# Gram stages of a two-block ResNet bottleneck: transposes moved from TensorE to a way through DRAM and VectorE

## The chip, the cores and the metric

The kernel runs on one core of one Trainium2 chip. The metric is the device time of one execution in microseconds (us), the median of several runs. The engines are TensorE (PE, matrix products and transposes into PSUM), VectorE (DVE), ScalarE (ACT), GpSimd (POOL) and SyncE (SP, which only issues DMA transfers). They run independently and wait for each other through semaphores.

## The reference

Two bottleneck blocks follow each other on x of shape (64, 1024, 14, 14), float32. Each block is

```python
out = relu(bn(conv(x, w1, b1, 1, 0), g1, be1))      # 1x1, 1024 -> 256
out = relu(bn(conv(out, w2, b2, 1, 1), g2, be2))    # 3x3, 256 -> 256
out = bn(conv(out, w3, b3, 1, 0), g3, be3)          # 1x1, 256 -> 1024
out = softplus(residual_scale)[0] * out
return relu(x + out)
```

`bn` takes mean and variance over all 64 x 196 = 12544 pixels of each channel in this very batch. So no normalisation can start before its convolution has ended for the whole batch, and the third convolution would have to be computed twice, or its output kept, unless its statistics are known ahead.

## The kernel before

All data are float32. 256 middle channels are two halves of 128 partitions (MS = 2), 1024 outer channels are eight (CS = 8). The batch is cut into T = 32 tiles of two images, PX = 392 pixels each. The output of the first convolution, and in its place that of the second, stays on the chip for the whole batch in `y_all`, 128 partitions x 2 x 12544.

The stages in order, with the times of the profile: the first convolution of block 0 (0 to 313 us); for each block the second convolution `conv2` (a Winograd form, 313 to 597 and 1340 to 1615), the Gram stage `gram` with `conv3_stats` behind it, and then the third convolution with the residual. For block 0 the latter is `fused` with the first convolution of block 1 (to 1340), for block 1 it is `final` (to the end).

The **Gram stage** finds the mean and variance of the third convolution without computing it. With z the normalised output of the second convolution (256 values per pixel), the variance of w3.z follows from the 256 x 256 matrix of the sums of z.z^T over pixels and the sums of z. `gram` (L855 on) goes through NT = 49 pairs of pixel tiles (2 x 128 pixels). For each it transposes four 128x128 blocks of `y_all` on TensorE into one PSUM bank (L885), VectorE copies the bank to an SBUF tile `zt` and takes off a row `crow` on the way (L887; this keeps the numbers small, c being relu of the norm's shift be2), and TensorE adds the products of the pair to two PSUM banks `g0` and `g1` (L867 and L868; a column of ones gives the sums). The products of a pair stand behind the transposes of the next. ScalarE normalises `y_all` in place ahead of it, group by group of GPX = 1568 pixels (`norm`, L487).

`conv3_stats` (L899 to L938) turns `g0`, `g1` and w3 into mean and variance of all 1024 channels; `affine` makes scale and shift of them; `residual` does tile 0.

Beside the Gram stage of block 0, GpSimd prepares the Winograd **filters** of block 1: four pieces (`filters`, L160 on; `piece` in the main loop), one per pair of channel halves, each with a load of w2, some 35 small operations (L171 to L206) and six stores to DRAM `us`. The filters of block 0 are prepared by VectorE in the first stage, half a piece per step of the first convolution (L1115 to L1124). Near the end of each Gram stage VectorE also makes sums and differences of w1 and w3 (`combine`, L135 to L142).

What sets the order: the program's order is a priority only. A planner with a model of the instructions' durations orders each engine's queue when the program is built; only where the code asks for it (`keep_in_program_order`: the convolutions' matmuls at L158, the activations at L278) is the order fixed. On the chip each engine works through its queue in that order and stops at an instruction whose data are not there. Tiles of a pool with the same tag share a number of buffers; a load into one waits until its last reader is done. SyncE issues most loads, ScalarE and GpSimd some; a transfer counts as landed when all of it is.

Of the kernel before, what the change touches and what calls it, by code (L numbers as in the profile page):

```python
# [33 lines left out]
FP = mybir.dt.float32  # L36
AF = mybir.ActivationFunctionType
ALU = mybir.AluOpType
# [13 lines left out]
CH = 2  # L52
NT = NPX // (CH * P)
NZT = 4

# [25 lines left out]

NROW = M


@with_exitstack
def bottlenecks(ctx: ExitStack, tc: tile.TileContext, x, w1s, w2s, w3s, pars, out):
# [7 lines left out]
    y_grp = y_all.rearrange("p s (g h l) -> p s g h l", g=NG, h=H)  # L94
    mids = [dram.tile([P, CS * PX], FP, tag=f"mid{t}", name=f"mid{t}") for t in range(T)]
    us = [
        [dram.tile([P, MS, MS, NKS[i], P], FP, tag=f"u{b}_{i}", name=f"u{b}_{i}") for i in range(NF)]
# [28 lines left out]

    def load_w1(pool, b):

        w = pool.tile([P, MS, 2, CS // 2, P], FP, tag="w1", name=f"w1_{b}")
        for h in range(2):  # L130
            for o in range(MS):
                nc.scalar.dma_start(out=w[:, o, h], in_=w1s[b][:, o, h])
        return w

    def combine(pool, name, a):  # L135

        s = [pool.tile(a[0][0].shape, FP, tag=f"{name}s{i}", name=f"{name}s{i}") for i in range(4)]
        tc.keep_in_program_order(nc.vector.tensor_add(s[0], a[1][0], a[1][1]))
        nc.vector.tensor_sub(s[1], s[0], a[0][0])
        tc.keep_in_program_order(nc.vector.tensor_sub(s[2], a[0][0], a[1][0]))  # L140
        nc.vector.tensor_sub(s[3], a[0][1], s[1])
        return a, s  # L142
# [13 lines left out]
    def matmul(*args, **kw):  # L156

        tc.keep_in_program_order(nc.tensor.matmul(*args, **kw))  # L158

    def filters(eng, b, s, o, spare):  # L160
# [24 lines left out]
        for i, (row, more, op, by) in parts.items():  # L185
# [23 lines left out]
            nc.gpsimd.dma_start(out=us[b][i][:, s, o], in_=u)  # L209
            if i == 2:  # L210
                yield

# [641 lines left out]

    def gram(psum, pool, aff, crow, beside):  # L855


        g0, g1 = psum.tile(M + 1, "cp"), psum.tile(P + 1, "ap")
        zts = [pool.tile([P, CH, M + 1], FP, tag=f"zt{i}", name=f"zt{i}") for i in range(NZT)]
        for zt in zts:  # L860
            nc.gpsimd.memset(zt[:, :, M:], 1.0)
        normed = 0

        def products(k, zt):
            for c in range(CH):
                first, last = k == 0 and c == 0, k == NT - 1 and c == CH - 1
                nc.tensor.matmul(g0, zt[:, c, 0:P], zt[:, c, :], start=first, stop=last)  # L867
                nc.tensor.matmul(g1, zt[:, c, P:M], zt[:, c, P:], start=first, stop=last)  # L868

        before = None  # L870
        for k in range(NT):
            while normed < NG and normed * GPX < (k + 3) * CH * P:

                px = [normed * GPX, (normed + 1) * GPX]
                if normed == 0:
                    px.insert(1, CH * P)
                for a, b in zip(px, px[1:]):
                    for s in range(MS):
                        norm(s, y_all[:, s, a:b], aff)
                normed += 1  # L880
            tp = psum.tile(CH * M)
            for c in range(CH):
                px = slice((k * CH + c) * P, (k * CH + c + 1) * P)
                for s in range(MS):
                    nc.tensor.transpose(tp[:, (c * MS + s) * P : (c * MS + s + 1) * P], y_all[:, s, px], ident)  # L885
            zt = zts[k % NZT]
            nc.vector.tensor_tensor(  # L887
                zt[:, :, :M], tp.rearrange("p (c m) -> p c m", c=CH),
                crow[:, None, :].to_broadcast([P, CH, M]), ALU.subtract,
            )  # L890
            if before is not None:
                products(*before)
            if k in beside:
                beside[k]()
            before = k, zt
        products(*before)
        return g0, g1

    def conv3_stats(psum, one, grams, w3, ccol, mv):  # L899

# [6 lines left out]
        nc.vector.tensor_scalar(off, g0[:, P:M], 2.0, None, ALU.mult)  # L907

        m = one.tile([P, MS, 2], FP, tag="zmean", name="zmean")
        for s, d in ((0, g0[:, M:]), (1, g1[:, P:])):  # L910
            nc.vector.tensor_copy(m[:, s, 1:2], d)
            nc.vector.tensor_add(m[:, s, 0:1], d, ccol[:, s : s + 1])
        quad = psum.tile(3 * CS, "ax").rearrange("p (o k) -> p o k", k=3)
        ones = one.tile([P, 1], FP, tag="ones", name="ones")
# [13 lines left out]
        for o in range(CS):  # L928
            for s in range(MS):
                matmul(quad[:, o, 0:2], w3[:, s, o, :], m[:, s, :], start=(s == 0), stop=(s == MS - 1))  # L930
        for o in range(CS):
            matmul(quad[:, o, 2:3], q[:, 0, o * P : (o + 1) * P], ones, start=True, stop=True)
        r = small.tile([P, CS, 3], FP, tag="quad", name="quad")
        nc.vector.tensor_copy(r, quad)
        nc.vector.tensor_copy(mv[:, :, 0], r[:, :, 0])
        sq = small.tile([P, CS], FP, tag="sq", name="sq")
        nc.vector.tensor_mul(sq, r[:, :, 1], r[:, :, 1])
        nc.vector.tensor_sub(mv[:, :, 1], r[:, :, 2], sq)  # L938

# [157 lines left out]
    with tc.tile_pool(name="first", bufs=1) as one, tc.tile_pool(  # L1097
        name="first_x", bufs=4
    ) as xpool, ExitStack() as scope:
        psum = Psum(scope, ["ps"], ps=4, ay=2)  # L1100
        w1 = load_w1(one, 0)
        pair = [load_x(xpool, 0, t, 4 if t == 0 else 2) for t in range(2)]
        for b in range(2):
            p = keep.tile([P, NPAR], FP, tag=f"par{b}", name=f"par{b}")
            nc.scalar.dma_start(out=p, in_=pars[b][:, :NPAR])
            par.append(p)
        masks.make_identity(nc, ident)
        w1 = combine_w1(one, w1)

        for t, xt in enumerate(pair):  # L1110
            plain_conv1(psum, t, xt, w1[0], par[0], stats1)


        spare = [y_all[:, i, NPX - CS * PX :] for i in range(MS)]
        quarters = itertools.product(range(MS), range(MS))  # L1115
        work = itertools.chain.from_iterable(
            itertools.chain(filters(nc.vector, 0, s, o, spare), (None,)) for s, o in quarters
        )

        def items():  # L1120
            for t in range(2, T, 2):
                xs = [load_x(xpool, 0, t + i) for i in range(2)]
                yield Conv1(psum, one, xs, (t, t + 1), w1, par[0], stats1)
                next(work, None)  # L1124

        for _ in stream(items()):
            pass

    for b in range(2):
        pb = par[b]  # L1130
        sp = softplus(pb)
        ccol = keep.tile([P, MS], FP, tag="ccol", name="ccol")
        nc.vector.tensor_scalar(ccol, pb[:, BE2 : BE2 + MS], 0.0, None, ALU.max)
        aff = affine(aggregate(stats1, T - 3 + b), MS, pb, G1, BE1)
# [4 lines left out]
        with tc.tile_pool(name=f"last_{b}", bufs=1) as one, tc.tile_pool(  # L1139
# [3 lines left out]
            if b == 0:  # L1143
                w1 = load_w1(one, b + 1)
            aff = affine(aggregate(stats2, 0), MS, pb, G2, BE2)
            with ExitStack() as scope:
# [4 lines left out]
                with tc.tile_pool(name=f"gram_{b}", bufs=1) as pool:  # L1151
                    crow = pool.tile([P, M], FP, tag="crow", name="crow")
                    nc.sync.dma_start(out=crow, in_=pars[b][:, NPAR:])
                    tc.keep_in_program_order(nc.vector.tensor_scalar(crow, crow, 0.0, None, ALU.max))

                    def piece(s, o):
                        spare = [xpool.tile([P, CS * PX], FP, tag="x", name="spare") for i in range(2)]
                        for _ in filters(nc.gpsimd, 1, s, o, spare):
                            pass

                    weights = []

                    def combined():
                        if b == 0:
                            weights.append(combine_w1(one, w1))
                        weights.append(combine_w3(one, w3))

                    beside = {NT - 5: combined}
                    if b == 0:
                        beside.update({1 + 12 * i: partial(piece, i // MS, i % MS) for i in range(MS * MS)})  # L1170
                    grams = gram(psum, pool, aff, crow, beside)
                    made = [conv3(psum, 0, o, w3) for o in range(2)]
                    mv3 = small.tile([P, CS, nc.vector.BN_AGGR_DIM], FP, tag="mv3", name="mv3")
                    conv3_stats(psum, pool, grams, w3, ccol, mv3)
                aff = affine(mv3, CS, pb, G3, BE3, conv_bias=B3)
# [51 lines left out]
```

## Time and profile before

The median is 2053.04 us of 3 runs (2052.73 to 2053.37). The profiled execution has a span of 2048.9 us.

| engine | busy us | share of the span |
|---|---|---|
| TensorE, matmuls | 1988.1 | 97% |
| TensorE, weight loads | 1679.1 | 82% |
| VectorE | 1559.7 | 76% |
| ScalarE | 906.4 | 44% |
| GpSimd | 664.2 | 32% |

| stage | from, to (us) | what is on TensorE |
|---|---|---|
| Gram stage of block 0 | 612 to 708 | transposes and products of 49 pairs |
| statistics, start of `fused` | 708 to 749 | `conv3_stats`, tile 0, first convolutions |
| Gram stage of block 1 | 1630 to 1722 | the same 49 pairs |
| statistics, start of `final` | 1722 to 1747 | as above |

How to read the profile: a group of instructions is given by its line, engine, operation and tile (out<-in), the number, the busy time in us and the mean of one in ns, and the idle time of the engine just before them with what ended it. The times of matmuls overlap, so a sum of them is more than the time they take; the distance from one to the next is the price. "PEclk" is the clock granted to TensorE, 1.00 being full. The chain of waits follows the work that ended last back from the end, at each step to what released it.

### The profile page before, as it was taken

What the parts mean: (1) busy time and instruction counts of PE and PEld (TensorE: products, weight loads), DVE (VectorE), ACT (ScalarE), POOL (GpSimd) and SP (SyncE); (2) the same over time, 40 slices, a digit from 0 to 9 for tenths busy, and PEclk for the clock granted to TensorE, in tenths of its full rate; (3) what the DMA queues carried; (4) which work ended last, traced back from release to release, by engine and by line L of the source; (5) the groups of instructions that cost most, each with busy time, mean ns of one, the idle gap of its engine ahead of it and who ended that gap; (6) DMA issues with size and microseconds to landing.
All of it is one profiled execution on the core that took longest, in us unless ns stands there. A gap on an engine that the chain in (4) does not pass through costs nothing.

```text
span 2048.9 us, 27957 instructions
## 1 busy us (share of the span) xinstructions
PE 1988.1 (97%) x9896; PEld 1679.1 (82%) x9896; DVE 1559.7 (76%) x2892; ACT 906.4 (44%) x1847; POOL 664.2 (32%) x736
## 2 busy tenths in 40 slices
PE   8989999999989979999999999999999899999998
PEld 4555557999989769999999999989999898555554
DVE  6875568999983556777677667699999734799997
ACT  1101114466644035555555555444656530555555
POOL 0100001121219964333333333312121100566665
PEclk9999999999999989999999999999999999999999
DMA  7755525565642254444444444255656420599998
GB/s 274 271 188 185 189 95 165 185 192 179 198 144 89 96 189 158 187 160 189 158 189 160 187 162 185 95 186 184 199 176 203 173 88 1 219 325 337 339 337 298
DMA packets 160890, 385.88 MB, mean 188 GB/s; under 512 B 8560, under 2 KB 129648, under 8 KB 144240
## 3 DMA queue, kind: packets, MB, share of 16 engines
q1 hardware_dynamic: 150720, 315.88, 44.5%
q10 hardware_dynamic: 5904, 51.91, 6.1%
q0 software_dynamic: 4128, 16.32, 2.0%
q8 instruction: 78, 1.28, 0.2%
q14 instruction: 60, 0.49, 0.1%
HBM read 268.21 MB, written 115.87 MB: 187 GB/s over the span
## 4 chain that ended last, share of the span: by engine, by line
PE 73%; DVE 12%; POOL 6%; DMA 4%; issue 3%; ACT 1%; SPq 0%; DVEq 0%; POOLq 0%; ACTq 0%
PE ay L158 14%; PE cy L158 13%; PE ap L158 7%; PE cp L158 6%; PE even L158 5%; PE odd L158 5%; PE m L158 5%; PE l L158 4%; PE ax L158 4%; PE cx L158 4%; POOL spare L171 3%; PE cp L867 2%; DVE x L404 2%; DMA x<-mid 2%; PE ps L158 1%
## 5 line engine op out<-in xcount | busy, mean ns | idle before, releaser
L278 ACT ACTIVATE cu<-cy,scale 128x196 f32<-128x196 f32 (+1 forms) x552 | 257.5, 475 | 297.5 <-PE cy L158 289.9
L543 POOL TENSOR_TENSOR diffs<-r 128x448 f32<-128x448 f32 (+1 forms) x80 | 111.3, 1402 | 616.9 <-DVE r L525 266.9
L278 ACT ACTIVATE x<-x,shift 128x392 f32<-128x392 f32 x368 | 211.9, 614 | 74.9 <-POOL x L430 58.7
L404 DVE SCALAR_TENSOR_TENSOR x<-cp,scale,x 128x196 f32<-128x196 f32 (+1 forms) x368 | 178.0, 484 | 83.1 <-PE cp L158 81.7
L158 PE MATMUL cy<-ct,w3s 128*128 128x196 f32 (+1 forms) x736 | 222.1, 383 | 2.5 <-ACT cu L278 2.5
L425 POOL TENSOR_TENSOR x<-x,cu 128x196 f32<-128x196 f32 (+1 forms) x184 | 167.3, 909 | 172.1 <-ACT cu L278 172.0
L158 PE MATMUL ay<-at,w1s 128*128 128x196 f32 (+1 forms) x752 | 209.7, 382 | 0.6 <-ACT au L278 0.6
L430 POOL TENSOR_TENSOR x<-x,cu 128x392 f32<-128x392 f32 x124 | 125.7, 1014 | 189.5 <-DVE x L404 189.4
L158 PEld LDWEIGHTS ay<-at,w1s 128*128 128x128 f32 x752 | 136.7, 191 | 35.0 <-ACT au L278 1.5
L158 PEld LDWEIGHTS cy<-ct,w3s 128*128 128x128 f32 x736 | 134.0, 191 | 36.9 <-ACT cu L278 4.1
L278 ACT ACTIVATE au<-ay 128x196 f32<-128x196 f32 (+1 forms) x141 | 53.9, 382 | 244.6 <-PE ay L158 223.2
L451 POOL TENSOR_TENSOR x<-x,cu 128x392 f32<-128x392 f32 x120 | 125.0, 1042 | 82.6 <-DVE x L404 77.5
L158 PE MATMUL m<-sums,ua 128*128 128x224 f32 (+1 forms) x752 | 145.5, 336 | 0.0
L158 PE MATMUL cy<-y,w 128*128 128x196 f32 (+1 forms) x416 | 131.2, 403 | 1.9 <-DVE x L948 1.9
L158 PEld LDWEIGHTS m<-sums,ua 128*128 128x128 f32 x752 | 131.4, 189 | 0.2
L404 DVE SCALAR_TENSOR_TENSOR x<-cx,scale,x 128x196 f32<-128x196 f32 (+1 forms) x184 | 89.1, 484 | 51.8 <-PE cx L158 51.6
L158 PE MATMUL cx<-y,w 128*128 128x196 f32 (+1 forms) x404 | 126.2, 398 | 0.0
L867 PE MATMUL cp<-zt 128*128 128x257 f32 x392 | 120.7, 390 | 5.4 <-DVE zt L887 5.4
L158 PE MATMUL even<-v,ub 128*128 128x224 f32 (+1 forms) x640 | 123.8, 334 | 0.8 <-ACT even L637 0.8
L158 PE MATMUL odd<-v,ub 128*128 128x224 f32 (+1 forms) x640 | 123.9, 335 | 0.2
L158 PE MATMUL l<-diffs,ub 128*128 128x224 f32 (+1 forms) x640 | 122.0, 333 | 0.0
L158 PE MATMUL cy<-ct,w 128*128 128x196 f32 (+1 forms) x368 | 111.2, 384 | 6.6 <-ACT cu L278 6.6
(230 smaller groups left out, 4430.4 us busy)
## 6 DMA issues: line engine op xcount, KB each, us to landing
x<-in_x SPq DMA_DIRECT2D x62, 1568.0 KB, 6.6
ub<-u SPq DMA_DIRECT2D x80, 768.0 KB, 4.6
x<-mid SPq DMA_DIRECT2D x32, 1568.0 KB, 10.2
mid<-x ACTq DMA_DIRECT2D x31, 1568.0 KB, 5.1
out<-x SPq DMA_DIRECT2D x124, 392.0 KB, 6.5
ua<-u SPq DMA_DIRECT2D x96, 256.0 KB, 2.9
ub<-u SPq DMA_DIRECT2D x16, 1024.0 KB, 6.1
u<-y POOLq DMA_DIRECT2D x20, 256.0 KB, 7.0
```

The costliest lines, as they stand in the source:

```text
L158: tc.keep_in_program_order(nc.tensor.matmul(*args, **kw))
L171: eng.tensor_scalar(to, v, by, None, ALU.mult)
L278: tc.keep_in_program_order(nc.scalar.activation(*args, **kw))
L404: nc.vector.scalar_tensor_tensor(v, bank, self.scale[:, o : o + 1], v, ALU.mult, ALU.add)
L425: nc.gpsimd.tensor_add(self.part(1, 1), self.part(1, 1), u3)
L430: nc.gpsimd.tensor_add(v, v, self.u12)
L451: nc.gpsimd.tensor_add(v, v, self.u12[:, i * self.n : (i + 1) * self.n])
L543: nc.gpsimd.tensor_sub(diffs, r[:, :, :, :WH], r[:, :, :, WH:])
L867: nc.tensor.matmul(g0, zt[:, c, 0:P], zt[:, c, :], start=first, stop=last)
```

## The change

In both Gram stages 36 of the 49 pairs are no longer transposed by TensorE. Their pixels are cut into STEPS = 9 steps of 1024 pixels. For each step, four transfers write the four bands of 32 partitions of `y_all` to DRAM (`out`), and four more bring them back (`back`) so that a band of 32 partitions holds all 256 channels of a run of 256 pixels. Then square blocks of 32x32, which is what VectorE's transpose does, are enough: four instructions per step (`by_vector`) write `zt` as the TensorE path does. The first FIRST = 9 pairs and the last LAST = 4 still go by TensorE (`by_tensor`), while the first step is on its way and at the end. "Out" runs four steps ahead and "back" two.

As `zt` no longer passes through a subtraction, c is taken off `y_all` itself behind the norm (`less`: ScalarE for whole groups in block 0, VectorE otherwise); the mean of the third convolution drops out of its normalisation, so the convolution can work on z less c too. `crow` and its load go, `conv3_stats` loses a few small operations, and `zt` has six buffers in place of four.

The tiles that the steps come back to (`homes`) are borrowed: the sums of w1 or w3, or a tile of the x pool. The filters of block 1 are shared out anew: one piece to VectorE in the first stage (five there, spread evenly over eleven steps of the convolution), one to VectorE beside the Gram stage in six parts, two on GpSimd. The load of w1 of block 1 moves from ScalarE's queue to SyncE's.

```diff
@@
-NT = NPX // (CH * P)
-NZT = 4
+NZT = 6
+
+FIRST, LAST = 9, 4
+RUN = 2 * P
+STEP = 4 * RUN
+STEPS = (NPX - (FIRST + LAST) * CH * P) // STEP
@@
+    zds = [dram.tile([32, MS, 4, STEP], FP, tag=f"zd{k}", name=f"zd{k}") for k in range(STEPS)]
@@ filters
-            if i == 2:
-                yield
+            yield
@@ gram
+        bounds = [0, CH * P, 3 * CH * P, *range(GPX, NPX + 1, GPX)]
+        for a, e in zip(bounds, bounds[1:]):
+            for s in range(MS):
+                y = y_all[:, s, a:e]
+                norm(s, y, aff)
+                less(s, y)
+
+        def out(k):
+            for j in range(4):
+                nc.sync.dma_start(
+                    out=zds[k][:, :, j], in_=y_all[32 * j : 32 * j + 32, :, start + k * STEP : start + (k + 1) * STEP]
+                )
+
+        def back(k):
+            x = homes(k)[:, : MS * STEP].rearrange("p (n f) -> p n f", f=RUN)
+            for j in range(4):
+                nc.sync.dma_start(
+                    out=x[32 * j : 32 * j + 32],
+                    in_=zds[k].rearrange("p s i f -> p (s i) f")[:, :, j * RUN : (j + 1) * RUN],
+                )
+            return x
@@
-            zt = zts[k % NZT]
-            nc.vector.tensor_tensor(
-                zt[:, :, :M], tp.rearrange("p (c m) -> p c m", c=CH),
-                crow[:, None, :].to_broadcast([P, CH, M]), ALU.subtract,
+            zt = next(zts)
+            nc.vector.tensor_copy(zt[:, :, :M], tp.rearrange("p (c m) -> p c m", c=CH))
+            return zt
+
+        def by_vector(x, i):
+            zt = next(zts)
+            nc.vector.transpose(
+                zt[:, :, :M].rearrange("p b (n c) -> p b n c", c=32),
+                x[:, :, i * CH * 32 : (i + 1) * CH * 32].rearrange("p n (b r) -> p b n r", r=32),
             )
+            return zt
+
+        def pairs():
+            for i in range(FIRST):
+                yield by_tensor(i * CH * P)
+            for k in range(STEPS):
+                x = ready.pop(0)
+                for i in range(RUN // (CH * 32)):
+                    yield by_vector(x, i)
+                if k + 4 < STEPS:
+                    out(k + 4)
+                if k + 2 < STEPS:
+                    ready.append(back(k + 2))
+            for i in range(LAST):
+                yield by_tensor(NPX - (LAST - i) * CH * P)
@@ the first stage
-        quarters = itertools.product(range(MS), range(MS))
+        pieces = [(0, 0, 0), (0, 0, 1), (0, 1, 0), (0, 1, 1), (1, 0, 0)]
@@
-                next(work, None)
+                if i < free:
+                    for _ in itertools.islice(work, total * (i + 1) // free - total * i // free):
+                        pass
@@ beside the Gram stage
+                    def less(k, y):
+                        if b == 0 and y.shape[-1] == GPX:
+                            nc.scalar.activation(y, y, AF.Identity, bias=minus_c[:, k : k + 1])
+                        else:
+                            nc.vector.tensor_scalar(y, y, minus_c[:, k : k + 1], None, ALU.add)
@@
-                    beside = {NT - 5: combined}
+                    beside = {FIRST + STEPS * RUN // (CH * 32): combined}
                     if b == 0:
-                        beside.update({1 + 12 * i: partial(piece, i // MS, i % MS) for i in range(MS * MS)})
+                        beside[1] = lambda: list(piece(nc.gpsimd, 0, 1))
+                        by_two = piece(nc.vector, 1, 0)
+                        beside.update({4 + 4 * i: partial(next, by_two) for i in range(NF)})
+                        beside[25] = lambda: list(piece(nc.gpsimd, 1, 1))
```

## The prediction

> **What bounds the kernel now.** I first cut the span into stages by the chain of waits, which names TensorE for 73%. The two stages that the change rewrites are the two Gram stages. This view gives each of them from the first normalisation to the last product, and then the stretch behind each, up to the steady stream of convolutions; the columns after the length are busy time and instruction count of TensorE, its weight loads, VectorE, ScalarE, GpSimd, then TensorE's granted clock, the DMA share and GB/s.
>
> ```profile
> 612.30:708.20 95.90, 90.12 (x588) 82.95 (x589) 41.29 (x59) 26.04 (x18) 86.57 (x135) 0.95 0.23 86
> 1629.70:1721.60 91.90, 90.32 (x589) 83.16 (x590) 36.65 (x55) 25.69 (x18) 0.00 (x0) 0.95 0.22 93
> 708.20:749.20 41.00, 30.68 (x126) 20.38 (x124) 23.71 (x53) 8.66 (x19) 38.51 (x59) 0.90 0.47 158
> 1721.60:1747.40 25.80, 25.27 (x95) 15.34 (x93) 13.61 (x41) 5.15 (x10) 0.00 (x0) 0.87 0.00 0
> ```
>
> TensorE fills both Gram stages; VectorE, ScalarE and the DMA are less than half used. The stretch behind the first one is 15 us longer than the same work behind the second, and its TensorE is idle for 10 us: GpSimd is busy all through it.
>
> The instructions of the second Gram stage by group (busy us, mean ns):
>
> ```profile
> L867 PE MATMUL cp<-zt 128*128 128x257 f32 x196 | 60.3, 389 | 0.8 <-DVE zt L887 0.8
> L868 PE MATMUL ap<-zt 128*128 128x129 f32 x196 | 38.3, 278 | 0.0
> L487 ACT ACTIVATE y<-y,shift,scale 128x1568 f32<-128x1568 f32 x14 | 22.3, 1679 | 0.0
> L887 DVE TENSOR_TENSOR zt<-cy,crow 128x512 f32<-128x512 f32 x25 | 17.3, 693 | 26.2 <-PE cy L885 26.1
> ...
> L885 PE MATMUL cy<-ident,y 128*128 128x128 f32 x100 | 16.4, 285 | 6.5 <-ACT y L487 6.5
> L885 PE MATMUL cx<-ident,y 128*128 128x128 f32 x96 | 15.4, 281 | 0.5 <-ACT y L487 0.5
> ```
>
> Matmuls overlap, so durations overstate their price. The pitch is read from the order in time, TensorE alone:
>
> ```profile
> 659.21 0.60 PE L885 MATMUL ay<-ident,y 128*128 128x128 f32 x4
> ...
> 659.65 0.60 PE L867 MATMUL cp<-zt 128*128 128x257 f32 x2
> ...
> 660.96 0.60 PE L885 MATMUL cy<-ident,y 128*128 128x128 f32 x4
> ```
>
> One pair of pixel tiles takes 660.96 - 659.21 = 1.75 us, of which four transposes take 659.65 - 659.21 = 0.44 us and the products 1.31. 49 pairs make 85.8 us; the rest is a cold start.
>
> The chain of waits where GpSimd holds up the stretch behind the first Gram stage:
>
> ```profile
> 742.77 1.83 POOL spare L171 x3
> 744.93 0.52 POOL u L209
> ...
> 746.06 0.61 POOL x L425
> 746.67 0.97 POOL x L430
> 747.69 0.50 issue
> 748.19 0.61 ACT x L278
> 749.16 1.02 PE cy L158 x2
> ```
>
> GpSimd ends its fourth filter piece at 745; the additions of the next convolution stand behind it in its queue, and TensorE has nothing from 742.5 to 749.2.
>
> [...] Nothing in this trace spans fewer than 128 partitions; those that do span them move 351 to 434 GB/s with several queued (434 and 431 in 1630 to 1640, 351 in 1748 to 1752). This is the question of the case. [...] granted clock 0.50 from 748 to 752, after the 6.6 us gap.
>
> **The change, part by part.**
>
> *Transposes on TensorE.* 36 of 49 pairs lose four: 36 x 0.44 = 15.8 us per Gram stage, all on the path.
>
> *Transposes on VectorE.* 36 of 128x512 in place of 36 subtractions of 693 ns. Bounds: 0.60 us (the pitch of such rows back to back, 704.11 to 704.71) and twice that; I take 0.70. At 2.8 us per step of four, against 5.24 us of products (4 x 1.31), it is hidden.
>
> *The way through DRAM.* 9 steps, each 1.05 MB out and 1.05 MB back, 18.9 MB per stage. Products of a step last 5.24 us, so the way must carry 400 GB/s in the steady part, or 18.9 MB in the whole time from the first "out" to the last step. Bounds: [...] 430 (this trace, 128 partitions) gives 44 us. [...] If the four quarters, which lie in one queue (SyncE issues one in 0.34 to 0.43 us)[...], do overlap, it comes near the full rate. I take 360 GB/s, 52.5 us, and know that this is the weakest number here.
>
> *Start of the way.* Step 0 needs pixels 2304 to 3328, so the third group of 1568. A pass of 1568 on ScalarE has a pitch of about 1.58 us (14 passes and 4 shorter ones in 26.0 us). First Gram stage: less c also runs on ScalarE, four passes or 6.3 us per group; group 0 takes some 4.4 us (an estimate from the same rows, cut in three pieces), so group 2 (counted from 0) is ready at 4.4 + 2 x 6.3 = 17.0 us after the first norm. Second: 4.4 + 2 x 3.15, plus some 1 us for less c on VectorE (L492 takes 0.63 us for 896 elements) = 11.7. Then out and back in turn, each about 4 to 4.5 us ([...]the trace lands 768 KB in 4.6): step 0 can be transposed at 26 and 20.5. TensorE has done its nine first pairs at about 19 (9 x 1.75 plus the cold start). So it **waits** 7 us in the first stage, and goes cold for another 2 us' loss; 1.5 to 2 us in the second. What queues behind this wait is every later product; nothing else of TensorE's can fill it.
>
> *Last step.* Transfers end at 17.0 + 52.5 + 2 = 71.5 and 11.7 + 52.5 + 2 = 66.2; then 5.2 for step 8 and 7.0 for the four last pairs: 84 and 78.4.
>
> *Sum for the Gram stages.* TensorE's path: 95.9 - 15.8 - 1 (no crow to load: L887's first waits 3 us on it) + 9 = 88 in the first, 91.9 - 15.8 - 1 + 2 = 77 in the second. The DMA end says 84 and 78. The later counts: 88 and 78, gains of 8 and 14.
>
> *Filters of block 1.* A piece costs about 33 us on GpSimd (617.4 to 647.7, 677, 709, 744) and 12.8 us on VectorE (51.1 us of filter rows for four in the first stage). GpSimd goes from four to two, done near 80 to 90 us after the first norm against 113 needed (88 + 25): the gap of 6.6 us and about 3 us of half clock behind it go, **gain 10**. The piece on VectorE fits: 36 x 0.7 + 13 x 0.69 + 13 = 47 us of 88.
>
> *First stage.* A fifth piece puts 12.8 us more on VectorE: per item of 18.4 us on TensorE, 11.9 of its own plus 30/11 x 2.1 = 5.8, total 17.7. It fits barely. Before, VectorE's wait of 6.8 us for "u<-y" at 111 cost TensorE some 5 us up to 130; with four boundaries between pieces in place of three I put 3 us more (bounds -4 and +10).
>
> *Statistics, w1's load on SyncE, no crow:* small, off or on the path by 1 us: -1.
>
> Total: -8 - 14 - 10 + 3 - 1 = -30: **2023 us**.
>
> **Rivals.** *The ports bound it* (ends slower): [...] At 215 (88 us): first stage 17 + 88 + 2 + 12.2 = 119, +23; second 114, +22; GpSimd's tail still goes, -10; first stage +3, rest -1: 2053 + 37 = **2090**[...]. For it: [...] the five x tiles (8 MB) that the second stage loads at its start now compete. [...] *Half bound:* 290 GB/s, 65 us: 96.2 and 90.8; +0.3 - 1.1 - 10 + 2: **2044**. *The gain is given back elsewhere:* the DMA keeps up but VectorE in order, filters and transposes in one queue, or the fifth piece cost 12 us more: **2035**. For it: GpSimd waits on VectorE's pieces to issue their stores; VectorE still has half the time free.
>
> **How the numbers follow.** Forecast (2010 to 2032) 0.40; given back or half bound 0.22; ports 0.38. The ports' case spreads from about 2060 to 2114; 2010 to 2088 leaves some 0.05 below and 0.15 above. Break-even is a rate near 255 to 260 GB/s. Faster 0.60, same 0.03, slower 0.37.
>
> **What would show it.** Right: a pitch of 1.31 us in the middle of both Gram stages, one gap of TensorE near the tenth pair, the DMA share near 0.9 with over 350 GB/s there, no gap at the start of the fused stage. Wrong: VectorE's transposes waiting on the transfers back at every step, 200 to 250 GB/s at a high DMA share, a broken clock. A VectorE transpose of over 1.3 us, or new gaps in the first stage, would also undo it.

## The result, and the profile after

The changed kernel takes **2077.05 us** (median of 4 runs, 2075.02 to 2078.60) against 2052.89 before on the same chip: 1.0121 times as long, 95% interval 1.0103 to 1.0138. The forecast of 2023 us with 0.60 for "faster" was wrong in its sign; the time lies inside the range, which was wide enough to hold the slow case too.

The stretches of the changed kernel that answer to those shown of before: both Gram stages from the first normalisation to the last product, and the stretch behind the first one (length; busy us and count of TensorE, weight loads, VectorE, ScalarE, GpSimd; granted clock, DMA share, GB/s):

```profile
613.80:730.60 116.80, 78.64 (x445) 69.65 (x446) 56.63 (x107) 47.49 (x34) 65.99 (x100) 0.86 0.89 261
1641.70:1745.30 103.60, 81.29 (x445) 71.98 (x446) 49.91 (x74) 26.57 (x20) 0.00 (x0) 0.89 0.91 263
730.60:763.00 32.40, 30.32 (x124) 20.21 (x122) 18.78 (x47) 8.77 (x19) 3.38 (x5) 0.89 0.38 146
```

TensorE has a quarter fewer instructions (445 in place of 588) and needs more time: 116.8 - 95.9 = +20.9 us and 103.6 - 91.9 = +11.7. The DMA share has gone from 0.23 to 0.9, the clock from 0.95 to 0.86 and 0.89. Between the Gram stages, from the last product of the first to the first norm of the second, it is 911.1 us against 921.5 (1641.7 - 730.6 and 1629.7 - 708.2), so -10.4; the first Gram stage starts 1.5 later, and what follows the second is 0.6 longer. The sum, +24.3, is the difference of the profiled spans (2073.2 - 2048.9). The loss lies wholly in the Gram stages.

What VectorE waits for in the first of them (us in all, times, longest):

```profile
DVE zt L913 <- DMA w1s<-zd: 16.4, 3, 6.7
DVE minus_c L1180 <- ACT y L1201: 16.3, 1, 16.3
DVE zt L913 <- DMA w3s<-zd: 14.2, 3, 5.8
```

and VectorE's transposes (L913) in the second, in order of time (start, length, in brackets the idle time before them and what ended it):

```profile
1670.63 2.49 DVE L913 STREAM_TRANSPOSE zt<-home 128x512 f32<-128x512 f32 x4 [1.29 <-DMA home<-zd]
1678.21 2.49 DVE L913 STREAM_TRANSPOSE zt<-w3s 128x512 f32<-128x512 f32 x4 [5.09 <-DMA w3s<-zd]
1688.25 2.49 DVE L913 STREAM_TRANSPOSE zt<-home 128x512 f32<-128x512 f32 x4 [7.54 <-DMA home<-zd]
1695.92 2.49 DVE L913 STREAM_TRANSPOSE zt<-w3s 128x512 f32<-128x512 f32 x4 [5.18 <-DMA w3s<-zd]
```

Four transposes take 2.49 us and then VectorE is idle until the next transfer back has landed, at every step but the last. From the first step's transposes (1670.63) to the eighth's (1723.14) are seven periods of 7.5 us where TensorE's products need 5.24. The ninth's start at 1733.77, though its transfer landed at 1728.6: VectorE has two copies for the last pairs and the sums of w3 ahead of them in its queue, the first of which waits for TensorE until 1730.0. TensorE stands still for 3.2 us there. SyncE's queue in the same stretch (start, time to issue all):

```profile
1654.44 7.41 SPq L885 DMA_DIRECT2D zd<-y  x8
1662.02 3.21 SPq L893 DMA_DIRECT2D home<-zd  x4
1665.33 3.46 SPq L885 DMA_DIRECT2D zd<-y  x4
1668.84 3.38 SPq L893 DMA_DIRECT2D w3s<-zd  x4
```

It issues without a pause, some 0.9 us per transfer (20 from 1654.44 to 1672.22). So the trace leaves two suspects open: the transfers themselves (bands of 32 partitions), or SyncE, which has eight of them to issue per step. A third was in the first stage. There TensorE stood still from 635.4 to 659.9, because the planner had put the transposes of the *last* pairs ahead of the first step's products ("PE ay L903 <- ACT y L1201" 24.4 us), and VectorE's first transposes stood behind `minus_c` of the *next* block (16.3 us above), which waits for the last subtraction on ScalarE.

### The profile page after: what moved, and what is told of

Same layout as the page of the kernel before. It is cut to its first block, busy times and chain, and to the rows that moved or that the text cites. A ratio compares the mean times of both kernels' runs of the same rounds, so it can differ in the third digit from the quotient of the medians.

```text
span 2073.2 us, 27603 instructions
## 1 busy us (share of the span) xinstructions
PE 1964.4 (95%) x9608; PEld 1652.4 (80%) x9608; DVE 1591.0 (77%) x2988; ACT 928.7 (45%) x1865; POOL 613.9 (30%) x658
## 4 chain that ended last, share of the span: by engine, by line
PE 67%; DVE 13%; DMA 8%; issue 4%; SPq 4%; ACT 2%; POOL 1%; DVEq 0%; POOLq 0%; ACTq 0%
PE ay L168 12%; PE cy L168 12%; PE ap L168 6%; PE cp L168 6%; PE even L168 5%; PE odd L168 5%; PE m L168 5%; PE l L168 4%; PE ax L168 4%; PE cx L168 3%; DMA x<-mid 3%; SPq L885 2%; PE cp L944 2%; DVE x L413 2%; SPq L893 2%
## 5 line engine op out<-in xcount | busy, mean ns | idle before, releaser
L552 POOL TENSOR_TENSOR diffs<-r 128x448 f32<-128x448 f32 (+1 forms) x80 | 112.4, 1416 | 585.4 <-DVE r L590 312.2
L944 PE MATMUL cp<-zt 128*128 128x257 f32 x392 | 125.6, 403 | 26.8 <-DVE zt L913 25.1
L168 PE MATMUL cp<-y,w3s 128*128 128x196 f32 (+1 forms) x368 | 113.7, 390 | 2.7 <-DVE x L413 1.3
## 6 DMA issues: line engine op xcount, KB each, us to landing
x<-mid SPq DMA_DIRECT2D x32, 1568.0 KB, 10.4
```

The source lines that it names most:

```text
L552: nc.gpsimd.tensor_sub(diffs, r[:, :, :, :WH], r[:, :, :, WH:])
L944: nc.tensor.matmul(g0, before[:, c, 0:P], before[:, c, :], start=first, stop=last)
```

## The experiments

Eighteen kernels. In e1, e2, e5, e9, e10 and e16 the pixels land in other places, so that their sums are not the Gram matrix; they serve the time alone. First all in one table: time, ratio to the kernel before with its interval, and where it bears on the argument the length of both Gram stages (95.9 and 91.9 before).

| kernel | us | ratio | Gram stages |
|---|---|---|---|
| changed | 2077.1 | 1.0121 (1.0103 to 1.0138) | 116.8, 103.6 |
| e1 all transfers 128 wide | 2034.9 | 0.9922 (0.9908 to 0.9937) | 94.1, 82.2 |
| e2 no transfers | 2013.6 | 0.9809 (0.9790 to 0.9828) | 82.9, 75.2 |
| e3 before, new filter sharing | 2045.2 | 0.9967 (0.9955 to 0.9979) | |
| e4 program order on TensorE | 2079.0 | 1.0143 (1.0124 to 1.0162) | 121.1, 102.9 |
| e5 128 wide, 1 KB runs | 2039.0 | 0.9939 (0.9924 to 0.9954) | 95.8, 85.0 |
| e6 back whole, out in eight | 2065.1 | 1.0069 (1.0052 to 1.0086) | |
| e7 the same, out spread | 2073.0 | 1.0103 (1.0088 to 1.0119) | |
| e8 out whole, back in bands | 2069.4 | 1.0086 (1.0070 to 1.0103) | |
| e9 out in bands, back wide | 2063.9 | 1.0054 (1.0037 to 1.0070) | 112.3, 93.9 |
| e10 back spread | 2077.4 | 1.0121 (1.0106 to 1.0136) | |
| e11 out for two steps, back whole | 2070.7 | 1.0085 (1.0067 to 1.0102) | 114.8, 98.4 |
| e12 e11 in program order | 2076.7 | 1.0112 (1.0095 to 1.0129) | |
| e13 bands 0, 2, 1, 3 | 2068.0 | 1.0086 (1.0072 to 1.0100) | 112.4, 97.7 |
| e14 e13 in program order | 2071.2 | 1.0103 (1.0089 to 1.0117) | |
| e15 e11 with bands 0, 2, 1, 3 | 2055.4 | 1.0026 (1.0016 to 1.0037) | 109.3, 90.5 |
| e16 out from bands 0, 1, 0, 1 | 2083.9 | 1.0170 (1.0155 to 1.0186) | 119.7, 109.1 |
| e17 e15, subtraction on VectorE | 2053.7 | 1.0013 (1.0007 to 1.0020) | 106.9, 89.9 |
| e18 e15 in the second stage alone | 2047.1 | 0.9980 (0.9971 to 0.9988) | 98.9, 90.9 |

The kernel before was timed again beside each group of runs and lies between 2050.6 and 2052.9. The ratio allows for that; a difference of two times from different groups can be off by some 2 us.

**e1, e2: is it the transfers, and how much?** What the recorded texts call "ports" is the theory that a band of 32 partitions limits a transfer; what in the hardware would do so, no run shows. In e1 each transfer spans 128 partitions:

```diff
-                    out=zds[k][:, :, j], in_=y_all[32 * j : 32 * j + 32, :, start + k * STEP : start + (k + 1) * STEP]
+                a = start + k * STEP + j % 2 * STEP // 2
+                nc.sync.dma_start(out=zds[k][:, j], in_=y_all[:, j // 2, a : a + STEP // 2])
...
-                    out=x[32 * j : 32 * j + 32],
...
+                    out=x[:, 2 * j : 2 * j + 2].rearrange("p n f -> p (n f)"), in_=zds[k][:, j]
```

> The changed kernel with each of its 72 + 72 transfers turned to span 128 partitions (512 pixels of one channel half, 2 KB runs) instead of 32 partitions; number, bytes and queue stay. It leaves the re-sorting of channels out, so the Gram sums are those of other blocks. Theory 'ports' (a band of 32 partitions limits a transfer): a step falls from 7.3 to near 5.3 us, the second Gram stage from 103.6 to about 84 us, the first from 117 to about 100, total near 2040. Theory 'issue' (SyncE takes 0.9 us for each transfer, whatever its shape): nothing changes, 2077 within 5.

e2 leaves all of them out and lets VectorE transpose pixels straight out of `y_all`.

> The changed kernel without the way through DRAM: VectorE transposes blocks straight out of y, so the Gram sums are of wrong blocks; all transfers out and back are left out. If TensorE's path is then the only limit, a pair costs 1.31 us in the middle, the second Gram stage takes 77 us and the first 80 to 88, total 2022 to 2030. If VectorE or the order of the queues were a limit of their own, it stays over 2045.

Both Gram stages of e1, then of e2:

```profile
616.70:710.80 94.10, 78.10 (x445) 69.79 (x446) 57.20 (x106) 47.47 (x34) 61.47 (x94) 0.89 0.86 317
1621.80:1704.00 82.20, 76.88 (x445) 68.84 (x446) 49.42 (x74) 26.60 (x20) 0.00 (x0) 0.93 0.87 322
```

```profile
616.50:699.40 82.90, 76.03 (x445) 68.21 (x446) 55.79 (x106) 47.46 (x34) 64.12 (x100) 0.94 0.43 157
1609.80:1685.00 75.20, 73.79 (x445) 66.73 (x446) 50.72 (x74) 26.60 (x20) 0.00 (x0) 0.95 0.27 114
```

The same instructions in other shapes of transfer are 42 us faster: 22.7 and 21.4 in the two stages. Without any transfer the stages take 82.9 and 75.2. So the whole loss, and the whole of the gain that didn't come, is in the way through DRAM.

**e4: does the order in the first stage matter?** TensorE's transposes and products in program order, and a `minus_c` tile per block.

```diff
-nc.tensor.transpose(...)
+tc.keep_in_program_order(nc.tensor.transpose(...))
...
-minus_c = keep.tile([P, MS], FP, tag="minus_c", name="minus_c")
+minus_c = keep.tile([P, MS], FP, tag=f"minus_c{b}", name=f"minus_c{b}")
```

> The changed kernel with TensorE's transposes and Gram products kept in program order and one minus_c tile per block, so that neither TensorE nor VectorE stands at a wait for the last group's 'less c' before the first step. Theory 'order' (24 us of idle TensorE in the first Gram stage comes from these two waits): first gap down from 24 to about 12 us, total near 2065. Theory 'transfers bind anyway' (the gap only moves, since the transfers end at the same time): 2077 within 4.

VectorE's first transposes in e4:

```profile
647.94 2.49 DVE L913 STREAM_TRANSPOSE zt<-w1s 128x512 f32<-128x512 f32 x4 [3.92 <-DMA w1s<-zd]
656.71 2.49 DVE L913 STREAM_TRANSPOSE zt<-w3s 128x512 f32<-128x512 f32 x4 [6.27 <-DMA w3s<-zd]
672.52 2.49 DVE L913 STREAM_TRANSPOSE zt<-w1s 128x512 f32<-128x512 f32 x4 [13.32 <-DMA w1s<-zd]
```

The long wait is gone and step 0 is transposed 14 us earlier (661.89 in the changed kernel); step 2 comes at 672.5 as before (672.95), and the last transfer back lands at 716.3 (716.7 in the changed kernel). What the order costs is time in which the transfers are behind anyway. The stage is even 4.3 us longer (121.1), as the last four pairs are now transposed at its end. The striking 24 us gap was not the cause.

**e3: the filters alone**, that is the kernel before with the new sharing of filter pieces.

> The kernel before, its Gram stages untouched, with only the new sharing of the filter pieces (five on VectorE in the first stage, one on VectorE and two on GpSimd beside the Gram stage). My steps: the gap behind the first Gram stage goes (-10), the first stage costs 3 more: 2046. Rival: VectorE's piece slows the copies of the Gram stage and the first stage loses more: 2053 or above.

The gain is 6.7 us, near the -10 and +3 of the forecast. In its trace the first Gram stage starts 2.7 us later than before (615.0), and from its last product to the second stage's first norm it is 8.4 us less. Of the kernels here that leave no part of the work out it has the lowest time.

**e5 and e8: SyncE?** How long SyncE takes to issue one (ns, least/median/most) in the changed kernel (L885, L893), then in e1 (L886):

```profile
L885 SPq DMA_DIRECT2D zd<-y x72: 565/740/2380, 630.6 to 1706.6; - x72
L893 SPq DMA_DIRECT2D home<-zd x20: 551/608/1397, 1662.0 to 1718.0; - x20
```

```profile
L886 SPq DMA_DIRECT2D zd<-y x72: 319/332/1246, 625.8 to 1673.0; - x72
```

A band of this form costs SyncE 0.55 us at least, a full-width transfer of e1 0.32, so e1 had relieved SyncE too. e5 keeps 128 partitions with three dimensions and 1 KB runs:

```diff
-                    out=zds[k][:, :, j], in_=y_all[32 * j : 32 * j + 32, :, start + k * STEP : start + (k + 1) * STEP]
+                a = start + k * STEP + j * RUN
+                nc.sync.dma_start(out=zds[k][:, j], in_=y_all[:, :, a : a + RUN])
```

> As many transfers as the changed kernel has, of the same bytes, in three dimensions and runs of 1 KB as its way back, but each over all 128 partitions (the pixels land in other places, so the Gram matrices are wrong; the work is the same). Ports theory: the width of a transfer sets the rate, so the time stays near that of the full-width transfers with 2 KB runs, 2035 to 2045. SyncE theory: the shape of the transfer makes SyncE's issue long (0.55 to 0.6 us each, against 0.32 for full-width rows), so that eight of them cost 4.8 us of a 5.2 us step; then 2065 to 2080 and issues of 0.55 us or more.

SyncE needs 0.36 us at least there and 0.50 in the median; the time is 2039.0. Not decisive alone, as the issue was again shorter. e8 is: one whole transfer out, so five issues per step in place of eight (each pair is transposed in two instructions).

```diff
-            for j in range(4):
...
-                    out=zds[k][:, :, j], in_=y_all[32 * j : 32 * j + 32, :, start + k * STEP : start + (k + 1) * STEP]
...
+            a = start + k * STEP
+            nc.sync.dma_start(
+                out=zds[k].rearrange("p (s f) -> p s f", s=MS), in_=y_all[:, :, a : a + STEP]
+            )
```

> Correct computation. The way out is one transfer over 128 partitions, the way back four bands of 32 partitions; VectorE transposes each pair in two instructions of half the size. Five issues per step. Ports theory: half the bytes at each rate, 6.3 us per step: 2055 to 2062. SyncE theory: five issues of about 0.6 us are 3 us per step and no bound: 2035 to 2045.

2069.4: **SyncE's issues are not the bound.** But the 2055 to 2062 of the other theory fell as well. Why, the traffic of 1660 to 1700 shows, one value per us, with SyncE's queue:

```profile
GB/s 208 204 237 411 418 338 202 208 220 211 370 418 406 442 397 328 201 216 219 244 411 401 367 206 214 218 249 360 412 371 254 230 241 276 346 402 396 302 257 277
```

```profile
1659.66 4.03 SPq L893 DMA_DIRECT2D w3s<-zd  x4
1663.79 1.22 SPq L885 DMA_DIRECT2D zd<-y  x2
1666.53 2.97 SPq L893 DMA_DIRECT2D home<-zd  x4
```

Two speeds take turns: 3 to 6 us at 400 GB/s, one or two whole ways out of 1.05 MB at 2.6 us each, and 4 to 5 us near 210, which are the four bands back. These bands run at half speed, 4.9 us for 1 MB, behind one whole way out or two.

The changed kernel has the same two speeds, with bands in both directions (660 to 700, one value per us):

```profile
GB/s 385 382 365 303 373 307 276 193 240 235 218 252 403 406 230 243 212 191 222 328 381 348 264 218 180 245 209 363 430 349 253 195 221 186 247 258 412 410 398 306
```

By the times of landing, the bands out of a step take mostly 2.5 to 3.5 us in the later steps of both stages and its bands back 4.4 to 5.2. From 1676.5 to 1681.5, with eight bands out under way, it is 381 GB/s; from 1682 to 1686.5, with four back, 219. So in the changed kernel the slow stretches are those in which the bands back land. That tells when the time goes, not yet why: in e9 below, with the way back at full width, the traffic still falls to between 158 and 291 GB/s for 3 to 4 us in each step (1667 to 1702).

**e6, e7, e9, e10, e11: which part of the way?** e6: way back whole, way out in eight bands of 128 KB, split by channel half. e7: the same, but a band is every fourth partition (`y_all[j::4]`), spread over all 128. e9: bands out as they are, back in four transfers 128 wide. e10: each quarter back goes to every fourth partition. e11: back whole, out for two steps at a time, in eight bands of 256 KB, so ten issues per two steps:

```diff
+            a, n = start + 2 * k * STEP, min(2, STEPS - 2 * k)
+            for j in range(4):
+                for s in range(MS):
+                    nc.sync.dma_start(
+                        out=zds[k].rearrange("(r q) s j f -> q s j r f", r=4)[:, s, j, :, : n * RUN],
+                        in_=y_all[32 * j : 32 * j + 32, s, a : a + n * STEP].rearrange("p (r f) -> p r f", r=4),
+                    )
```

> Correct computation. The way back is one transfer over 128 partitions in runs of 8 KB; the way out stays in bands of 32 partitions, cut into eight. Ports theory: half of the bytes move at the full-width rate (about 2.6 us per step), the other half at the band rate (3.7 us): a step of 6.3 us in place of 7.3, so some 9 us less per Gram stage: 2055 to 2062. SyncE theory: nine issues per step in place of eight, so no better: 2075 to 2085.

> Correct computation. The way back is one transfer over 128 partitions; the way out takes every fourth partition (32 partitions spread over all 128) in place of 32 neighbours, eight transfers of 1 KB runs. Ports theory: [...]a step near TensorE's 5.2 us, 2030 to 2045. If the number of partitions of a transfer counts, not which: as with bands out and the whole way back, within 5 us of that run. SyncE theory: nine issues per step, 2075 to 2085.

> The way out as in the changed kernel, four bands of 32 partitions; the way back in four transfers over all 128 partitions in runs of 2 KB (the same number, the same bytes; the pixels land in other places, so the Gram matrices are wrong). With the way out whole and the way back in bands, the traffic alternated between about 400 GB/s and 205 to 220. Theory now: the slow leg is the write into 32 partitions alone, so this comes near the run with all transfers at full width: 2035 to 2045. Rival: bands cost the same in both directions; then half of the excess stays: 2055 to 2060.

> As the changed kernel, with each quarter of the way back written to every fourth partition (32 partitions spread over all 128) in place of 32 neighbours (the blocks are wrong, the work is the same). If it counts which partitions a transfer writes: 2035 to 2045. If it counts how many: 2072 to 2082, with phases of 205 to 220 GB/s as before.

> Correct computation. The way back is one transfer over 128 partitions per step; the way out takes two steps at a time, in eight bands of 32 partitions and 256 KB, so SyncE issues ten transfers per two steps in place of sixteen. Theory (only writes into 32 partitions are slow, and with eight small ways out per step SyncE was the next limit): 2035 to 2048, faster than before. If bands out are slow as well: 2055 to 2065.

e9 (2063.9): both directions suffer; my view that only writes into 32 partitions are slow fell, and e11 with it (2070.7). The two do not add up: full width out gains 8 us (e8), full width back 13 (e9), both 42 (e1). e10 (2077.4) and e7 (2073.0): spreading a band over all partitions gains nothing. (e10 is the better test: in e7 SyncE also needs 0.61 us per issue, against 0.47 in e6.) e6 (2065.1) ends 3 us above the range of either half of the loss cured, its eight small ways out keeping SyncE at work (0.47 us each in the median). e12 is e11 with the order of e4:

> Correct computation. The run before with TensorE's transposes and products in the order of the program and a tile of its own for the subtracted term of each block. With the transfers bound, this order changed nothing. If the transfers now keep up, the early gap of TensorE in the first Gram stage (10 us in the full-width run) counts: 5 to 10 us below the run before, 2028 to 2042. If they do not keep up: within 3 us of it.

6 us above e11: again no gain from that order.

**e13 to e16: the order of the bands.** In the order 0, 1, 2, 3 the neighbours 0 and 1 lie in the lower half of the partitions, 2 and 3 in the upper. In e11, where each band goes in two transfers, four in a row share a half. e13 has one edit, in both directions:

```diff
-            for j in range(4):
+            for j in (0, 2, 1, 3):
```

> The changed kernel, correct, with one edit: the four bands are issued in the order 0, 2, 1, 3, out and back, so that neighbours in the queue lie in different halves of the partitions. Theory: [...]transfers in one queue overlap only with their neighbours, and in the order 0, 1, 2, 3 neighbours share a half (phases of 205 to 220 GB/s, broken by 400 where band 1 meets band 2 and band 3 the next band 0). Alternated, the rate comes near the full-width one: 2032 to 2048, over 340 GB/s in the steps. Rival: a narrow transfer is slow whatever its neighbour: 2072 to 2082.

> Correct computation. Whole way back over 128 partitions, way out for two steps at a time in eight bands (2070.7 with bands in order), now in the order 0, 2, 1, 3. Theory of the halves: 2032 to 2050. Rival: unchanged, 2067 to 2074.

For e15 the loop over the channel halves goes outside, so that neighbours in the queue always change halves. The traffic of e11 from 1670 to 1690 and of e15 from 1656 to 1676 (one value per 0.5 us), each with the issues:

```profile
GB/s 307 346 367 373 305 246 197 227 336 383 393 406 397 414 410 381 377 356 324 295 270 320 291 262 221 188 221 205 180 266 270 234 213 201 221 217 197 197 201 139
```

```profile
1668.07 18.45 SPq L887 DMA_DIRECT2D zd<-y  x15
```

```profile
GB/s 43 88 203 303 322 354 375 377 340 258 209 231 344 385 395 406 406 410 406 402 410 406 406 406 402 410 397 410 410 402 393 377 373 363 236 137 156 223 289 313
```

```profile
1656.22 14.67 SPq L887 DMA_DIRECT2D zd<-y  x15
```

In both, the two whole ways back issued just before these bands land some 9 us after their issue, by 1676.4 in e11 and by 1664.6 in e15; behind that the bands out are alone. In order, from 1682 on, they move some 180 to 270 GB/s (216 on average to 1689.5, at a DMA share of 0.8 or more in every half us, so the engines are held and not short of issues); alternated, from 1665.5 to 1671, 390 to 410. The bytes and the count are the same. That is shown, then, for these stretches: **of bands out that go alone, four in a row that share a half run at half speed; alternated between the halves, the same bands run at the full speed.** e16 below agrees: there eight bands out in a row lie in the lower half, to the same places in DRAM as in the changed kernel, and after some 4 us (353 GB/s, 1681 to 1685) the traffic falls to 203 (1685 to 1688).

It is no rule for every stretch. The changed kernel's bands out, two in a row per half and behind bands back, reached 381 GB/s without alternation, and with the first eight of e15's first stage under way, alternated, all traffic was only 285 to 303 (632.5 to 640). What else counts, such as what stands ahead in the queue, was not tested. The second Gram stage of e15 takes 90.5 us against 98.4.

e13 gained 9 us (7 by the ratios), less than expected, and the traffic says where (1665 to 1705, one value per us):

```profile
GB/s 434 349 219 267 220 251 308 413 414 422 415 321 242 218 251 266 381 421 381 262 234 260 321 399 379 348 250 255 287 386 393 318 350 239 289 323 404 390 305 257
```

```profile
1667.34 6.48 SPq L885 DMA_DIRECT2D zd<-y  x8
1673.86 2.78 SPq L893 DMA_DIRECT2D home<-zd  x4
1676.74 3.11 SPq L885 DMA_DIRECT2D zd<-y  x4
```

Against the issues and some 5 us to landing, the bands out are the stretches at 380 to 420 and the bands back those at 220 to 270. The bands out were as fast in the changed kernel. What alternation shortened is the way back: from 1665 to 1705 the traffic is below 300 GB/s for 4 to 6 us per step there and for 2 to 4 here. It doesn't cure the way back, nor does spreading it (e10). A way back at full width gains 13 us by itself (e9), and with alternation it brings the kernel to 2055 (e15). The bands back also read DRAM in runs of 1 KB that lie 4 KB apart, in e8 too, which no full-width way back here does. Whether that or the 32 partitions hold them up **stays open**.

> The run before, with TensorE's transposes and products in program order and a tile of its own for the subtracted term of each block. If alternation makes the transfers keep up, TensorE's early gap in the first Gram stage counts, and this gains another 3 to 8 us: 2026 to 2042; if it doesn't, within 4 us of the run before.

> As the changed kernel, but the way out reads bands 0, 1, 0, 1 in place of 0, 1, 2, 3 (the same bytes; half of the channels are taken twice, so the Gram matrices are wrong). Theory of the halves: six of the eight transfers of a step now lie in the lower half, 1.57 MB at some 215 GB/s = 7.3 us, plus a part of the other two (2.4 us) that overlaps at its ends alone: a step of 8.2 to 9.5 us in place of 7.3, 2090 to 2115. Rival (narrow transfers are slow whichever half they lie in): 2072 to 2082.

e14 is 3 us above e13: no gain. e16 puts six of eight transfers into the lower half: 6.8 us slower than the changed kernel (10 by the ratios), beyond the rival's 2082 but short of the 13 us or more of the theory. The direction fits, my estimate of how little the two other bands overlap didn't.

**e17, e18: what is left of the idea.**

```diff
-                        if b == 0 and y.shape[-1] == GPX:
+                        if False:
```

> The best correct version so far (bands in the order 0, 2, 1, 3, whole way back; 2055.4), with the subtraction in the first Gram stage on VectorE in place of ScalarE, as in the second stage. The forecast put step 0 at 17 us after the first norm for that work on ScalarE, and 11.7 where it is on VectorE. If the start of the way sets the end of the first stage, it gains the 5 us: 2048 to 2052. If VectorE, with the filter piece and the transposes in one queue, takes it back, or the rate alone sets the end: 2054 to 2058.

```diff
+            for i in range(total - LAST if inside else FIRST):
...
+            for k in range(0 if inside else STEPS):
```

> The best correct version so far with the way through DRAM in the second Gram stage alone; the first transposes all pixels on TensorE (and still subtracts with ScalarE). There the way cost 109.4 us against 95.9 before; the second stage took 90.6 against 91.9. Expected: 13 us less than 2055.4, so 2040 to 2046, about the 2045 of the new sharing of the filters alone, since the way through DRAM then gains no more than 1 to 3 us. If the transposes by VectorE were worth their 14 us in the second stage, it would be near 2031.

e17: the first stage is 2.4 us shorter (106.9), half of the 5 us; the kernel's ratio (1.0013 against 1.0026) moved by no more than the two intervals allow for chance. The late start is a small part. e18: 2047.1, no faster than the filters alone (2045.2). With both cures, the way through DRAM gains 1 us in the second stage (90.9 against 91.9), and 13 are lost where it is taken in the first (109.3 against 95.9). Why the first stage loses so much more was not settled; with no transfers (e2) it takes 82.9.

## Why the prediction was wrong, step by step

- *Transposes on TensorE, -15.8 per stage:* right. Less 1 for `crow`, the forecast gave TensorE's path 79.1 and 75.1 us without waits; e2 has 82.9 and 75.2.
- *Transposes on VectorE, 0.70 us:* right. 0.67 each, four in 2.49 us, hidden.
- ***The way through DRAM*, 360 GB/s: this step failed.** From the first issue to the last landing the 18.9 MB took 86.1 and 74.1 us, that is 219 and 255 GB/s, where the forecast had 52.5 and 2 (the 2 an estimate for one transfer; in the trace before, 256 KB land in 2.9 us and 768 KB in 4.6, `ua<-u` and `ub<-u`, medians). All traffic together is 285 and 275 GB/s from 660 to 720 and 1668 to 1728, with a DMA share above 1. At full width (e1) the way took 72.1 and 57.6 us, and all traffic is 388 (660 to 700) and 371 (1650 to 1690). So of the 31.6 and 19.6 us too many, the bands account for 14.0 and 16.5; the rest stays at full width too. No trace of before had a band of 32 partitions. I leaned on the rates of the wide transfers there (351 to 434 GB/s), hoping that four bands in one queue would overlap; the 360 was my estimate. In the steps of the changed kernel the transfers out come near that, at 2.5 to 3.5 us per MB; those back, at 4.4 to 5.2, do not. The slow stretches here lie mostly at 180 to 250, those of e8 at 200 to 220. It is not the price of every band: alternated, many in the queue, they reach 390 to 410 (e15). And spreading 32 partitions over all 128 gains nothing (2077.4 in e10, 2073.0 in e7 against 2065.1 in e6).
- *Bytes:* the forecast divided 18.9 MB by the rate and put the other traffic at nothing. The stages move 261 x 116.8 = 30.5 MB and 263 x 103.6 = 27.2; the rest is filters and x tiles. The x tiles of the second stage, which arrived at its start before, are now issued behind the last way back (from 1719 on), so they did not slow the way, which the rival had feared.
- *Start of the way:* "out" began 16.8 and 12.8 us after the first norm (17.0 and 11.7 forecast): right. Out and back then took not 9 us: step 0 was transposed at 661.9 - 613.8 = 48.1 and 1670.6 - 1641.7 = 28.9, against 26 and 20.5. The second is the transfers (two ways out are queued ahead of the first way back); the first is the order as well, which e4 showed to be harmless. That TensorE restarts "cold" shows in both traces: its granted clock is 0.50 from 612.3 to 618.0 before, behind an idle time of 7.3 us, and 0.50 from 659.9 to 664.0 in the changed kernel, behind the gap from 635.4 on.
- *Last step, 12.2:* 11.7 and 11.5 from the last step's first transpose (730.6 - 718.9, 1745.3 - 1733.8). From the last landing, where the forecast began to count, 13.9 and 16.7, as VectorE's queue held the last transposes up in the second stage. Thus the second stage is 28.9 + 7 x 7.5 + 10.6 + 11.5 = 103.5.
- *Filters -10, first stage +3:* right: -10.4 between the stages, +1.5 up to the first norm, and e3's -6.7.
- *Break-even near 255 to 260 GB/s:* by the sum's own terms it is a way of 69.4 us, near 272 GB/s: the stages then take 31.2 + 69.4 = 100.6 and 25.9 + 69.4 = 95.3, 8 us more than before in all, which is what the other terms gain.

Of the rivals "the ports bound it" came nearest: it gave 2090 at 215 GB/s, a rate that no trace of before showed; the measured 2077 came with a way at 219 and 255. That the bands are the reason is shown only in part (e7, e9, e10). "Half bound", at 290 GB/s, gave 2044: its rate was above that of the way, and it kept the forecast's early first step and counted no other bytes. "Given back elsewhere" has a small share, the 3.2 us for which VectorE's queue stops TensorE before the ninth step.

## What to carry to other kernels

Price a DMA by the shape it has, not by the best rate in the trace: here bands of 32 partitions ran at 200 to 220 GB/s in their slow stretches and the mix at 275 to 285, beside 371 to 388 at full width, and the rate needed was 400. Count all bytes of the stage, too: even at full width the way took 72 and 58 us in place of 52.5. Where bands can't be avoided, try neighbours of the queue in different halves of the partitions (15 us from e11 to e15, 12 by the ratios), and make the other direction whole. And before a long wait is called the cause, ask what the step after it waits for: removing the 24 us gap of TensorE gained nothing, as the transfers behind it were just as late.

## What the runs showed of the hardware that I had not expected

- Alternating the halves took bands out that go alone from 216 GB/s on average (e11) to 390 to 410 (e15), with the same count and bytes.
- Spreading 32 partitions over all 128 gained nothing: 2077.4 us in e10 against 2077.1 in the changed kernel, 2073.0 in e7 against 2065.1 in e6.
- What SyncE needs at least to issue 256 KB depends on the form of the transfer, not on its width alone: 0.55 us for the changed kernel's bands, 0.30 for those of e11, which hold one channel half, 0.32 (e1) and 0.36 (e5) at full width. e8's whole way out, 1.05 MB, needs 0.55.
- The DMA share stands near 1 at 200 GB/s as at 400: in the changed kernel 223 GB/s from 1720 to 1727 and 427 from 1729 to 1740, at 1.19 and 1.01. It tells that the engines are held, not what they move.
